# Values of 256 key rows by seven block products, in the setup of a graph-attention kernel

## The chip, the cores and the metric

The kernel runs on one core of a Trainium2 chip. The metric is device time in microseconds of one execution; a run lists several executions, and the median is used. The core's engines run side by side, each through its own queue in the order in which the program issues to it: TensorE (PE in the profile; PEld is its weight load), VectorE (DVE), ScalarE (ACT), GpSimd (POOL) and SyncE (SP, which here only issues DMAs). They wait for one another through semaphores. SBUF and PSUM are the on-chip memories; matmuls write to PSUM, and DVE or ACT copy from there.

## The reference

A graph-attention layer: 16 graphs of 512 nodes with 512 features, 16 heads of 32, and attention from every node to the first 20 nodes, in two directions (d = 0, 1).

```python
def _gat_attention(self_feat, cond_adj, label_bias, Wq, bq, Wk, bk, Wout, bout):
    B, N, F = self_feat.shape
    ng = min(NONGT, N)
    dh = F // H
    kv = self_feat[:, :ng]
    qh = (self_feat @ Wq.T + bq).reshape(B, N, H, dh)
    kh = (kv @ Wk.T + bk).reshape(B, ng, H, dh)
    aff = jnp.einsum('bnhd,bmhd->bnhm', qh, kh) * (1.0 / np.sqrt(dh))
    mask = cond_adj[:, :, None, :] > 0
    aff = jnp.where(mask, aff, NEG) + label_bias[:, :, None, :]
    w = jax.nn.softmax(aff, axis=-1)
    out_t = jnp.einsum('bnhm,bmf->bnhf', w, kv)
    out = jnp.einsum('bnhf,hgf->bnhg', out_t, Wout) + bout.reshape(H, F // H)
    return out.reshape(B, N, F)
...
        vcq = jnp.concatenate([exp_v, q_exp], axis=-1)
        self_feat = vcq @ W_self.T + b_self
        output = self_feat
        for d in range(2):
            ...
            output = output + _gat_attention(self_feat, cond, vb, Wq[d], bq[d], Wk[d], bk[d], Wout[d], bout[d])
        rel = jax.nn.relu(output)
        return exp_v + rel
```

The kernel exchanges the order of the last two products: it makes the values `kv @ Wout` of the 16 x 20 = 320 key rows once, in the setup, for both directions. Each is a product of 320 rows by 512 inputs with a 512 x 512 matrix. Half of `bout[0] + bout[1] + b_self` is added to the values of each direction.

## The kernel before

**Stages.** A setup (to about 86 us) loads the weights, makes the features of the 320 key rows (`kvn`, and `kvT` with its bias), the key vectors `khD`, the transformed keys `g` (16 head groups by 304 columns, stored to DRAM as `g_d`, the first two graphs kept in `gg`), the key biases `cq`, the values `vw_d`, and the first graph's own features. Then a loop over 16 graphs follows, in which PE makes scores, attention sums and the next graph's features. All matmuls are float32. A matmul of 64 or 32 output rows uses a part of PE's columns, so two or four of them run beside one another, and each float32 matmul leaves two records in the trace.

**Order.** The schedule is manual: the order of the calls in the program is the order in each engine's queue. The framework adds the semaphores, by tile and region; a tile taken from a pool again waits for all readers of the tile that held the buffer before.

**Rounds of the setup.** A loop over `n` = 0 to 12 (the last part of the listing) calls `keys(n)` and then the matmuls of one gap, by one letter each out of `plan[n]`. `keys(n)` issues a burst of small matmuls (line 949) on the tiles `s0`, `s1` and `t2` of PSUM, ordered by `bursts`, and the copies of their results to a tile `st`: ACT first (line 970), then DVE (line 972) and ACT (line 973). All three PSUM tiles have one buffer, so the next burst waits for these copies. Where a tile `st` is complete, POOL copies a part to `gg` (line 977) and SP stores the rest. The burst covers units (fc, hg, d, m), 46 of them in round 0, 41 in round 1, 46 in round 2; a unit needs `khD` of (d, hg).

The letters of a gap: `k` is `key_rows`, 16 matmuls whose result DVE copies to `khD` (line 850, `key_end`); `m` is `bias_terms`, a DVE product of `wq_sb` and `br_sb` with an accumulated sum (line 858); `v` and `w` are single steps of the values (line 902); `b` makes the biases `bqbd` on DVE and ACT; `c` is `bias_scores` (matmul, ACT copy, four POOL DMAs); `n` is `row_flags`; `p` is `block_product`, a block of the first graph's own features. Ahead of the loop four of the eight `key_rows` are made; the remaining four are (0, 2), (1, 2), (0, 3), (1, 3), in this order.

**Values before.** `values(t, ds, k)`: for each of the row blocks t = 0, 1 (128 rows) and each direction, four steps k over the 512 inputs, a step being two matmuls of 64 rows with 512 columns into one PSUM bank; then the last 64 rows with both directions in one bank. `value_pieces` adds the bias on DVE from the finished bank (line 918) and stores from POOL (line 922). The bias tile `br_sb` is completed on POOL at the end of round 2 by adding both rows of `bout` (line 1045), after the last `bias_terms` has read it.

**POOL ahead of the rounds.** `row_sums(0)` (lines 213 and 215) adds the four blocks of the first graph's `x`, which arrives during round 0, then `own_rows` and two copies to `c` follow, then the copies to `gg`.

**Buffers.** The pool `sfp`, tag `sf`, has three buffers: `wk0`, `wk1` and `kvD` hold them until the last `key_rows`; later come `rx1` (`row_sums(1)`, round 5), `sf0` and `t0` (round 8). The tag `adj` has three: `adj0_0`, `adj0_1`, the piece `v11`, then later masks. PSUM banks `acc0` and `acc1` (function `bank`) serve keys, values, bias scores, flags and block products in turn.

## Time and profile before

| | us |
|---|---|
| median of 3 executions | 544.9 |
| lowest, highest | 544.53, 545.13 |
| profiled execution, its own time | 546.22 |
| its span, first to last instruction | 544.2 |
| granted PE clock over the span | 0.997 |

Busy time by stage, in us of each stretch:

| stretch | PE | DVE | ACT | POOL | DMA share |
|---|---|---|---|---|---|
| 25 to 30 | 5.00 | 3.32 | 2.06 | 3.54 | 1.07 |
| 35 to 40 | 5.00 | 4.67 | 2.11 | 0.74 | 1.00 |
| 55 to 60 | 5.00 | 2.32 | 2.72 | 4.83 | 0.99 |
| 100 to 200 | 100.00 | 93.42 | 86.08 | 89.49 | 0.69 |
| 520 to 545 | 18.16 | 18.28 | 11.26 | 15.72 | 0.35 |

How to read it: a row of a timeline gives start, duration, engine, line, operation and the tiles written and read, with a count where neighbours are merged; in square brackets stands the idle time of that engine just before, and what ended it. A duration runs from an instruction's start on its engine to its end, so time for which it is held back on the engine is in it. The first and the last instructions of a stretch may be counted in two stretches. Times on POOL are rough.

### The profile page before, as it was taken

To read this page: it belongs to the slowest core of one execution; us is meant where nothing else is said; L and a number is where in the kernel's file an instruction comes from. 1 tells how busy PE (TensorE), PEld (TensorE's weight loads), DVE (VectorE), ACT (ScalarE), POOL (GpSimd) and SP (SyncE) were. 2 spreads that over 40 slices of the span, in tenths; PEclk is the share of its full clock that TensorE was granted. 3 is DMA by queue.
4 is the path that set the end of the run, shared out by engine and by line. 5 is a ranking of instruction groups with operands and counts; after the bars stand their busy time and mean duration, and the time that the engine had idled before them with its cause. 6 is when DMAs were issued, how large, how long until landed. Compare 5 with 4: busy or idle time off the path is not lost.

```text
span 544.2 us, 19643 instructions
## 1 busy us (share of the span) xinstructions
PE 537.1 (99%) x7932; PEld 427.1 (78%) x7932; DVE 472.3 (87%) x694; ACT 410.2 (75%) x1003; POOL 445.2 (82%) x447
## 2 busy tenths in 40 slices
PE   9999999999999999999999999999999999999995
PEld 5554469999887878887878788788888787888783
DVE  1785567899999999999999998999999999999996
ACT  1236646988887878797988888888888787877663
POOL 2657887679999897979797979898989989797584
PEclk9999999999999999999999999999999999999998
DMA  8999999476676877677767767576757676645024
GB/s 304 379 402 377 321 333 354 141 212 218 201 222 199 230 206 227 198 214 216 231 199 212 220 182 231 179 236 190 234 182 228 204 207 203 202 122 161 3 78 182
DMA packets 96182, 120.29 MB, mean 221 GB/s; under 512 B 20732, under 2 KB 64540, under 8 KB 94044
## 3 DMA queue, kind: packets, MB, share of 16 engines
q1 hardware_dynamic: 94748, 116.89, 67.9%
q0 software_dynamic: 768, 1.36, 1.2%
q8 instruction: 63, 1.03, 0.8%
q10 hardware_dynamic: 576, 0.79, 0.4%
q14 instruction: 27, 0.22, 0.2%
HBM read 83.41 MB, written 36.90 MB: 221 GB/s over the span
## 4 chain that ended last, share of the span: by engine, by line
PE 97%; DVE 1%; ACT 0%; issue 0%; DVEq 0%; ACTq 0%
PE ps_f L665 32%; PE ps_a L395 24%; PE ps_c L395 11%; PE ps_d L395 6%; PE ps_o_f L567 5%; PE ps_g L949 4%; PE ps_v L902 3%; PE ps_k L841 3%; PE ps_kv L784 2%; PE ps_a L282 1%; PE ps_o_c L567 1%; PE ps_l L395 1%; PE ps_c L282 1%; PE ps_kv L738 1%; PE ps_o_s L567 0%; PE ps_nz L220 0%
## 5 line engine op out<-in xcount | busy, mean ns | idle before, releaser
L325 ACT ACTIVATE prod<-adj,wb_sb 128x80 f32<-128x80 int32 x330 | 116.0, 429 | 0.0
L535 POOL TENSOR_TENSOR w<-w,sm 128x640 f32<-128x640 f32 x63 | 80.3, 1274 | 31.4 <-DVE sm L531 28.4
L665 PE MATMUL ps_f<-t,ws_s 128*64 128x246 f32 x720 | 80.1, 370 | 0.0
L665 PEld LDWEIGHTS ps_f<-t,ws_s 128*64 128x64 f32 x720 | 52.8, 136 | 18.0
L526 ACT ACTIVATE w<-w 128x640 f32<-128x640 f32 x60 | 43.8, 731 | 17.7 <-DVE w L522 17.7
L543 DVE STREAM_TRANSPOSE wt<-w 128x640 f32<-128x640 f32 x63 | 52.5, 833 | 0.1
L665 PE MATMUL ps_f<-x,ws_v 128*64 128x246 f32 x480 | 52.4, 371 | 0.0
L530 DVE TENSOR_REDUCE sm<-w 128x32 f32<-128x640 f32 x63 | 51.1, 811 | 0.1
L521 DVE TENSOR_REDUCE ps_d<-w 128x32 f32<-128x640 f32 x59 | 48.7, 826 | 1.8 <-ACT ps_d L429 0.2
L522 DVE TENSOR_TENSOR w<-w,ps_d 128x640 f32<-128x640 f32 x59 | 48.4, 821 | 2.0
L665 PEld LDWEIGHTS ps_f<-x,ws_v 128*64 128x64 f32 x480 | 35.4, 137 | 12.3
L368 POOL TENSOR_TENSOR k<-gg,k 128x608 f32<-128x608 f32 x30 | 44.7, 1489 | 0.0
L395 PEld LDWEIGHTS ps_a<-gg,sf 128*64 128x64 f32 x544 | 34.4, 137 | 5.8 <-issue 5.8
L970 ACT ACTIVATE st<-ps_g 128x448 f32<-128x448 f32 (+5 forms) x25 | 14.6, 642 | 32.1 <-PE ps_g L949 22.1
L395 PE MATMUL ps_a<-gg,sf 128*64 128x152 f32 x544 | 38.7, 295 | 0.0
L336 DVE TENSOR_REDUCE add<-prod 128x80 f32<-128x960 f32 x32 | 36.7, 1146 | 1.6 <-POOL prod L331 0.9
L395 PE MATMUL ps_d<-gg,sf 128*64 128x152 f32 x544 | 38.0, 293 | 0.0
L344 ACT COPY both<-add 64x80 f32<-64x80 f32 x128 | 32.6, 255 | 6.0 <-DVE add L336 4.9
L567 PE MATMUL ps_o_c<-wt,ve 32*32 32x256 f32 (+1 forms) x480 | 35.9, 386 | 0.0
L680 POOL TENSOR_TENSOR t<-x,t 128x492 f32<-128x492 f32 x30 | 34.9, 1162 | 1.2
L395 PEld LDWEIGHTS ps_d<-gg,sf 128*64 128x64 f32 x544 | 35.4, 137 | 0.2 <-ACT sf L683 0.2
L680 POOL TENSOR_TENSOR t<-x 128x492 f32<-128x492 f32 x30 | 34.9, 1164 | 0.0
(187 smaller groups left out, 1464.4 us busy)
## 6 DMA issues: line engine op xcount, KB each, us to landing
g_d<-st SPq DMA_DIRECT2D x16, 1064.0 KB
gg<-g_d SPq DMA_DIRECT2D x56, 304.0 KB
out_T<-o SPq DMA_DIRECT2D x60, 256.0 KB
x<-in_xT SPq DMA_DIRECT2D x56, 256.0 KB
xn<-in_xn SPq DMA_DIRECT2D x48, 256.0 KB
adj<-in_adj SPq DMA_DIRECT2D x52, 220.0 KB
nz<-nz_d SPq DMA_DIRECT2D x14, 256.0 KB
adj<-in_adj SPq DMA_DIRECT2D x6, 440.0 KB
```

The lines of the kernel that those rows point to most:

```text
L325: nc.scalar.activation(p[:, :, l], a[:, :, l], AF.Identity, scale=wb_sb[:, l : l + 1])
L368: done["ksum"] = engine.tensor_sub(to, one, two)
L395: nc.tensor.matmul(slot(g)[bass.ts(p, P // 2), : HL * S].rearrange("p (h m) -> p h m", m=NG)[:, :, 1:], of(k)[:, bass.ds(first + g * P // ...
L521: nc.vector.tensor_reduce(mx, f, AX.X, ALU.max)
L522: done["weigh"] = (engine or nc.vector).tensor_sub(f, f, mx.unsqueeze(2).to_broadcast([P, per, NG]))
L526: done["exp"] = nc.scalar.activation(t, t, AF.Exp)
L530: nc.vector.tensor_reduce(sm, heads(weighs[b, c, l]), AX.X, ALU.add)
L535: done["normal"] = nc.gpsimd.tensor_mul(f, f, smalls.pop((b, c, l)).unsqueeze(2).to_broadcast([P, per, NG]))
L543: done["turn"] = nc.vector.transpose(wts[b][:, c, l], weighs.pop((b, c, l)).rearrange("p g w -> p (g w)"))
L567: nc.tensor.matmul(outsum[b][a][bass.ds(at // 2 * DH, n * DH), bass.ds(c * N // 2 + lo * R, (hi - lo) * R)].rearrange("p (n r) -> p n r", ...
L665: nc.tensor.matmul(parts[b][n in (2, 3, 5)][bass.ts(a, P // 2), bass.ts(i, HN)], lhs, x[:, k], start=False, stop=k == 1, skip_group_check= ...
L680: done["xsum"] = nc.gpsimd.tensor_sub(to, one, two)
```

## The change

The first 256 key rows, with both directions at once, are one product of a 256 x 512 matrix (rows t = 0, 1; inputs in two halves j) with a 512 x 1024 matrix (halves j; directions d). Taken as 2 x 2 blocks, it is made by the seven products of Strassen's method in Winograd's form. Each product is two steps of two matmuls with 512 columns. It needs sums of blocks:

- `value_sums`: four sums of blocks of `kvT` on DVE, three in round 0 and one in round 1, right after `keys(n)`, of 256 columns each; three go into a new tile `kvS` of the tag `adj`, the fourth over a block of `kvT`.
- `weight_blocks`: four differences of blocks of `wo_sb`, 1024 columns each. Numbers 1, 2 and 4 run on POOL at the ends of rounds 1, 2 and 4, number 3 on DVE in two halves at the ends of rounds 3 and 4. They go into new tiles `wt0` and `wt1` of the tag `sf`.
- `value_product` accumulates product 2 in bank `acc1`, products 1, 6, 7, 4 one on another in `acc0`, and 5, 3 in a new `acc1`, in the order 2, 1, 5, 6, 3, 7, 4. `value_pieces` now runs once at the end of a round; it adds the bias into slices of a new tile `vs` (tag `sf`), joins the sums from PSUM on DVE, and stores.

The two rows of `bout` are added to one another on POOL at the end of round 1, and one sum completes `br_sb` in round 2. `bias_scores` is called in gaps 6 and 7 in place of 5 and 6. The warm-up matmuls at the start have 192 columns in place of 208. The last 64 rows are made as before.

```diff
+        kvS = load.tile([P, 2, S * L], F32, tag="adj", name="kvS", bufs=3)
+        kvS = kvS.rearrange("p t w -> p (t w)")[:, : 6 * P].rearrange("p (i k r) -> p i k r", i=3, k=2)
+        vx, vw = {}, {}
...
-            unit = nc.const_aps.tensor(1.0, [P, 208], F32)
+            unit = nc.const_aps.tensor(1.0, [P, 192], F32)
             for _ in range(4):
-                nc.tensor.matmul(warm[:, :208], unit[:, :P], unit, start=True, stop=True)
+                nc.tensor.matmul(warm[:, :192], unit[:, :P], unit, start=True, stop=True)
...
+            def weight_blocks(n, engine=nc.gpsimd, ks=slice(0, 2)):
+
+                b11, b21, b12, b22 = (wo_sb[d][:, 2 * j : 2 * j + 2] for d in range(2) for j in range(2))
+                if n == 1:
+                    t = [sfp.tile([P, C, F], F32, tag="sf", name=f"wt{i}") for i in range(2)]
+                    vw.update({1: b11, 2: b21, 3: b22, 5: t[0][:, :2], 6: t[0][:, 2:], 7: t[1][:, :2], 4: t[1][:, 2:]})
+                    vw["to"] = sfp.tile([P, C, F], F32, tag="sf", name="vs")
+                to, one, two = {
+                    1: lambda: (vw[5], b12, b11), 2: lambda: (vw[6], b22, vw[5]),
+                    3: lambda: (vw[7], b22, b12), 4: lambda: (vw[4], b21, vw[6]),
+                }[n]()
+                engine.tensor_sub(to[:, ks], one[:, ks], two[:, ks])
+
+            def value_sums(n):
+
+                a11, a12, a21, a22 = (kvT[:, 2 * j : 2 * j + 2, bass.ts(t, P)] for t in range(2) for j in range(2))
+                s1, s2, s4 = (kvS[:, i] for i in range(3))
+                if n == 0:
+                    nc.vector.tensor_add(s1, a21, a22)
+                    nc.vector.tensor_sub(s2, s1, a11)
+                    nc.vector.tensor_sub(s4, a12, s2)
+                else:
+                    nc.vector.tensor_sub(a21, a11, a21)
+                vx.update({1: a11, 2: a12, 3: s4, 4: a22, 5: s1, 6: s2, 7: a21})
+
+            def value_product(n, k):
+
+                first, i = n in (1, 2, 5), int(n in (2, 5, 3))
+                if first and k == 0:
+                    vw["ps", i] = bank(f"ps_v{n}", i)
+                for a in range(2):
+                    half = bass.ts(a, P // 2)
+                    nc.tensor.matmul(
+                        vw["ps", i][half], vx[n][:, k, half], vw[n][:, k],
+                        start=first and k == 0, stop=k == 1, skip_group_check=True,
+                    )
+                if k == 1:
+                    ended.append(n)
...
+                for n in sorted(done_now, key=(2, 1, 5, 6, 3, 7, 4, 0).index):
+                    if n == 2:
+                        with_bias(to[0], other)
+                    if n == 1:
+                        nc.vector.tensor_add(to[0], own_ps, to[0])
+                        store_values(to[0], 0, (0,))
+                    if n == 5:
+                        with_bias(to[1], other)
+                    if n == 6:
+                        with_bias(to[2], own_ps)
+                    if n == 3:
+                        nc.vector.tensor_add(to[2], other, to[2])
+                        store_values(to[2], 0, (1,))
+                    if n == 7:
+                        nc.vector.tensor_add(to[1], own_ps, to[1])
+                        store_values(to[1], 1, (1,))
+                    if n == 4:
+                        with_bias(to[3], own_ps)
+                        store_values(to[3], 1, (0,))
...
-                "v": [(values, (t, (d,), k)) for t in range(2) for d in range(2) for k in range(C)],
-                "w": [(values, (2, (0, 1), k)) for k in range(C)],
+                "v": [(value_product, (n, k)) for n in (2, 1, 5, 6, 3, 7, 4) for k in range(2)],
+                "w": [(values, (k,)) for k in range(C)],
             }
-            plan = "kmmk kmmmk mmmvvv vvv vvvb cvvv vvvc vnw www np pp pp pp".split()
+            plan = "kmmk kmmmk mmmvvv vvv vvvb vvv vvc cww wwn np pp pp pp".split()
...
                 keys(n)
+                if n < 2:
+                    value_sums(n)
...
-                    value_pieces()
                 if n == 2:
-                    for d in range(2):
-                        nc.gpsimd.tensor_add(br_sb, br_sb, bo_rows[d])
+                    nc.gpsimd.tensor_add(br_sb, br_sb, bo_rows[0])
+                value_pieces()
+                if n == 1:
+                    nc.gpsimd.tensor_add(bo_rows[0], bo_rows[0], bo_rows[1])
+                    weight_blocks(1)
+                if n == 2:
+                    weight_blocks(2)
+                if n in (3, 4):
+                    weight_blocks(3, nc.vector, slice(n - 3, n - 2))
+                if n == 4:
+                    weight_blocks(4)
```

`with_bias(v, ps)` is the DVE operation of line 918 (half of `br_sb` plus the bank), and `store_values(v, t, ds)` holds the POOL DMAs of line 922; both were parts of `value_pieces` before.

More of the change, by code (lines that the diff above doesn't have):

```diff
@@ L891, in gat_kernel @@
             ended = []
-            def values(t, ds, k):
+            def weight_blocks(n, engine=nc.gpsimd, ks=slice(0, 2)):
[9 more added lines that the diff above has]
+                engine.tensor_sub(to[:, ks], one[:, ks], two[:, ks])
@@ L896, in values, with store_values @@
+            def values(k):
+                if k == 0:
+                    vw["ps", 2] = bank("ps_v", 0)
+                for d in range(2):
+                    nc.tensor.matmul(
+                        vw["ps", 2][bass.ts(d, P // 2)], kvT[:, k, 2 * P :], wo_sb[d][:, k],
+                        start=(k == 0), stop=(k == C - 1),
+                    )
+                if k == C - 1:
+                    ended.append(0)
+            def store_values(v, t, ds):
                 rows = min(P, BM - t * P)
-                if k == 0:
-                    held[1 + t // 2] = bank(f"ps_v{t}{ds[0]}", int((t, ds) == (0, (1,))))
@@ L899, in values @@
-                ps = held[1 + t // 2]
                 for i, d in enumerate(ds):
-                    for a in range(2 * rows // P):
-                        nc.tensor.matmul(
-                            ps[bass.ds(i * rows + a * P // 2, P // 2)], kvT[:, k, bass.ds(t * P + a * P // 2, P // 2)], wo_sb[d][:, k],
-                            start=(k == 0), stop=(k == C - 1),
-                        )
-                if k == C - 1:
-                    ended.append((t, ds, ps))
+                    edge = EARLY * NG
@@ new lines, in store_values, with with_bias @@
+                    for n, lo, hi in ((0, 0, edge), (1, edge, rows)) if t == 0 else ((1, 0, rows),):
+                        nc.gpsimd.dma_start(
+                            vw_d[n][d, :, bass.ds(t * P + lo - n * edge, hi - lo)].rearrange("c r w -> r c w"),
+                            v[bass.ds(i * rows + lo, hi - lo)].rearrange("p (c w) -> p c w", c=C),
+                        )
+            def with_bias(v, ps):
+                nc.vector.scalar_tensor_tensor(v, br_sb, 0.5, ps, ALU.mult, ALU.add)
@@ L909, in value_pieces @@
             def value_pieces():
[L911 to L925 removed]
+                done_now = set(ended)
@@ new lines, in value_pieces @@
+                ended.clear()
+                to = [vw["to"][:, i] for i in range(C)] if "to" in vw else None
+                other, own_ps = vw.get(("ps", 1)), vw.get(("ps", 0))
+                for n in sorted(done_now, key=(2, 1, 5, 6, 3, 7, 4, 0).index):
[17 more added lines that the diff above has]
+                        store_values(to[3], 1, (0,))
+                    if n == 0:
+                        v = msk.tile([P, H * S], F32, tag="full", name="v2")[:, :F]
+                        with_bias(v, vw["ps", 2])
+                        store_values(v, 2, (0, 1))
```

15 lines of the change are left out of this document (removed).

## Prediction

> **What bounds the kernel now.** I read the page first, for which engine the chain of waits ends on.
>
> ```profile
> span 544.2 us, 19643 instructions
> PE 537.1 (99%) x7932; PEld 427.1 (78%) x7932; DVE 472.3 (87%) x694; ACT 410.2 (75%) x1003; POOL 445.2 (82%) x447
> PE 97%; DVE 1%; ACT 0%; issue 0%; DVEq 0%; ACTq 0%
> ```
>
> PE is busy for 99% of the span, and 97% of the chain lies on it. So a microsecond of matmul taken away counts in full, and a microsecond for which PE waits is added in full. Next I read PE's timeline where the values are made.
>
> ```profile
> 25.58 4.30 PE L841 MATMUL ps_k<-kvD,wk 128*32 128x304 f32 x64
> 29.81 1.39 PE L949 MATMUL ps_g<-khD,wq_sb 32*128 32x176 f32 x24
> 31.14 4.30 PE L841 MATMUL ps_k<-kvD,wk 128*32 128x304 f32 x64
> 35.37 1.54 PE L949 MATMUL ps_g<-khD,wq_sb 32*128 32x128 f32 x32
> 36.83 2.79 PE L902 MATMUL ps_v<-wo,kvT 128*64 128x512 f32 x12
> 39.56 1.66 PE L949 MATMUL ps_g<-khD,wq_sb 32*128 32x112 f32 x32
> 41.15 2.79 PE L902 MATMUL ps_v<-wo,kvT 128*64 128x512 f32 x12
> 43.88 1.63 PE L949 MATMUL ps_g<-khD,wq_sb 32*128 32x160 f32 x32
> ```
>
> Columns: start, duration, engine, line, matmul, count. Each row starts where the one before it ends: PE has no idle time here. Rounds alternate: a burst of key products (L949), then a gap (as the code calls it) of other matmuls. Round 1 begins at 29.81, round 2 at 35.37, round 3 at 39.56.
>
> **Matmuls removed.** Three steps of `values` (12 records) run from 36.83 to 39.56: 2.73 us, 0.91 a step. The sixteen steps for the first 256 rows become seven products of two steps with the same 512 columns: fourteen. Two steps go: **-1.82 us**. The last 64 rows keep four steps; bias scores change place, not count.
>
> **Warm-up.** 4 x 16 columns fewer.
>
> ```profile
> 0.84 3.11 PE L738 MATMUL ps_kv<-const-float32-1.0 128*128 128x208 f32 x8 [0.84 <-PEq L1421]
> 3.88 0.29 PEld L784 LDWEIGHTS ps_kv<-xkv,ws_v 128*64 128x64 f32 x4 [0.49 <-DMA ws_v<-in_wsT]
> ```
>
> The warm-up would be 3.11 x 16/208 = 0.24 us shorter, but the first real weights are loaded at 3.88, after 0.49 us of waiting for their DMA. The DMA stays: I count 0, bounds 0 and -0.24.
>
> **New work on DVE and POOL: how the two share.** The added sums take both inputs from SBUF, on both engines. The trace has that meeting.
>
> ```profile
> 25.34 1.22 DVE L972 TENSOR_SCALAR st<-ps_g 128x608 f32<-128x608 f32 x2 [0.63 <-PE ps_g L949]
> 26.30 1.28 POOL L213 TENSOR_TENSOR rx<-x 128x512 f32<-128x512 f32 x1 [4.27 <-DMA x<-in_xT]
> 27.67 2.96 POOL L215 TENSOR_TENSOR rx<-rx,x 128x512 f32<-128x512 f32 x2
> 27.91 0.59 DVE L850 TENSOR_SCALAR khD<-ps_k,bk_sb 128x304 f32<-128x304 f32 x1 [1.34 <-PE ps_k L841]
> 28.42 1.08 DVE L858 SCALAR_TENSOR_TENSOR bqt<-wq_sb,br_sb 128x512 f32<-128x512 f32 x1
> 29.43 1.75 DVE L858 SCALAR_TENSOR_TENSOR bqt<-wq_sb,br_sb 128x512 f32<-128x512 f32 x1
> L858 DVE SCALAR_TENSOR_TENSOR bqt<-wq_sb,br_sb x8: 680/686/1748, 28.4 to 38.9; 128x512 f32<-128x512 f32 x8
> 87.49 1.50 POOL L680 TENSOR_TENSOR t<-x 128x492 f32<-128x492 f32 x1
> 88.12 1.43 DVE L382 TENSOR_TENSOR f<-f,sf 128x512 f32<-128x512 f32 x1
> ```
>
> A `bqt` product takes 0.68 us (minimum of eight), but 1.75 at 29.43, ending only after POOL's sum does (30.63). At 88.12 a DVE sum whose first input was just made on DVE waits in the same way for POOL's, which ends at 88.99. So the two take turns, a whole instruction each, even where DVE's operations stand back to back. The khD copy, with one input in PSUM, keeps its 0.59 beside POOL's sums.
>
> [...]
>
> **First wait: three sums in round 0.** `value_sums(0)` is queued on DVE behind the eviction that ends at 26.56 and ahead of khD for (0, 2). That khD is read by the burst of round 1: round 0 takes the first 46 units, round 1 starts on the next, and its 11 shared ones are (0, 2). Before, khD ends at 28.50 for a burst at 29.81: 1.31 us to spare. Each sum has 256 columns. No row shows that size; the 512-column product runs in 0.68 and a 304-column sum in 0.69 with its tail. Bounds 0.2 and 0.69; I take 0.33, half of 0.68. Alone they would make 1.0 us and fit. But POOL makes the row sums from 26.30 on. The first waits until 27.59 and ends at 27.92; POOL takes 1.2 (29.12); the second ends at 29.45; POOL to 30.65; the third at 30.98; khD 0.59 to 31.57. Burst 1 starts near 31.6: **+1.8** (bounds 0.9, if DVE comes first, and 2.4).
>
> **Second wait: the weight sums in rounds 1 and 2.**
>
> ```profile
> 23.51 3.08 SPq L1029 DMA_DIRECT2D bo<-in_bout x2
> 32.90 0.82 POOL L977 COPY gg<-st 128x304 f32<-128x304 f32 x2
> 33.46 0.59 DVE L850 TENSOR_SCALAR khD<-ps_k,bk_sb 128x304 f32<-128x304 f32 x1 [0.64 <-PE ps_k L841]
> 36.50 1.22 DVE L972 TENSOR_SCALAR st<-ps_g 128x352 f32<-128x352 f32 x2
> 38.63 0.61 POOL L977 COPY gg<-st 128x304 f32<-128x304 f32 x1 [4.91 <-ACT st L973]
> 39.87 2.63 POOL L1045 TENSOR_TENSOR br_sb<-br_sb,bo 128x512 f32<-128x512 f32 x2 [0.64 <-DVE bqt L858]
> 42.73 0.69 DVE L918 SCALAR_TENSOR_TENSOR v<-br_sb,ps_v 128x512 f32<-128x512 f32 x1 [0.59 <-POOL br_sb L1045]
> ```
>
> POOL was idle for 4.91 us before 38.63, while DVE made five `bqt`s undisturbed. Into that idle time go one bias sum (half of 2.63: 1.28) and the first weight sum of 1024 columns. No row has 1024; twice 1.28 is 2.5, bounds 1.5 (the 608-column rate with a shorter tail) and 3.2. Their inputs, issued by 26.6, are read without a wait at 39.87; no row shows them late for POOL's turn, so I let them be there. Counted on from burst 1 at 31.6: it ends at 32.9, key products at 35.05 and 37.15, burst 2 at 38.6, three value steps at 41.33. On DVE: two `bqt`s, khD and the round's eviction to 34.6, the new sum to 34.95, khD to 35.75. POOL copies `gg` to 35.2 and makes the bias sum to 36.5; one `bqt` ends at 37.1; POOL makes the weight sum to 39.5; two `bqt`s and khD to 41.1; the eviction of burst 2 (1.22) ends at 42.35. Burst 3 writes the same PSUM and starts at 42.45 in place of 41.33: **+1.1**.
>
> Then come three `bqt`s with a `gg` copy (2.0, to 44.3), POOL's one remaining bias sum (to 45.7), 0.23 until DVE starts (42.50 to 42.73 in the rows), and the bias of the second product, 0.69, to 46.6. Product 5 takes that bank at once and could start at 44.96 (burst 3, one step): it starts near 46.7: **+1.75** (bounds of these two waits together 1.5 and 4).
>
> If round 1 isn't late, POOL's weight sum still stands between the `bqt`s: eviction of burst 2 at 41.3 for 39.56 (1.8), bias at 45.45 for a start at 43.9 (1.65): 3.45.
>
> **What I cost at nothing.** The biases of products 5, 6, 4 and the joins of 1, 3, 7 (0.69 each, one input in PSUM) end before their banks are wanted: two operations a round in a round of 4.3, of which evictions take 1.3. The two halves of the third weight sum on DVE (0.68 each) fall where POOL issues DMAs or copies; behind POOL's mask product they would cost up to 1.0. Weight sums two and four, 2.5 each, make POOL's queue longer:
>
> ```profile
> 72.42 1.15 POOL L255 TENSOR_TENSOR t<-x,t 128x492 f32<-128x492 f32 x1
> 74.37 1.83 PE L282 MATMUL ps_a<-t,ws_s 128*64 128x246 f32 x16
> ```
>
> The x sum for that product ends 0.8 us before it. POOL had gaps of 2.4 us ahead of it, and PE comes 2.8 us later by my sum: 0, with 0.8 as the upper bound. The row sums, x sum tiles and stores now share the `sf` buffers with the new tiles; the stores out of `vs` are issued two rounds before the tile is rewritten. Bias scores a round later have only stores behind them, which are read many rounds after. On SP nothing is moved.
>
> **Sum.** -1.82 + 1.8 + 1.1 + 1.75 = +2.8 us. The profiled execution took 546.2 us around its span of 544.2, and would take 549.0; the median of the three runs is 1.3 lower, 544.9, so I forecast **547.7**. Its own range is 546.2 to 549.2.
>
> **Rivals.**
> 1. *Only the weight sums collide.* The three sums slip in before POOL's. For: 0.25 us decides whether DVE or POOL is first at 26.3. Against: POOL was first, and x's landing is not moved. -1.82 + 3.45: 546.5.
> 2. *Only round 0 stalls.* POOL's weight sum finds a slot between evictions. Against: five `bqt`s in a row. -1.82 + 1.8: 544.9.
> 3. *Nothing stalls, the other side.* One mechanism: DVE keeps its turn while it has operations queued. Then the three sums end by 27.59 + 1.0 = 28.6 and khD by 29.2, and the `bqt`s end before the weight sum starts. It decides at khD by 29.7 and the second product's bias by 42. For: the sums alone fit the 1.34 us of idle time before khD. Against: the rows at 29.43 and 88.12. 543.1.
> [...]
> 5. *POOL's queue and the halves on DVE cost their bounds.* 0.8 + 1.0 more: 549.5.
>
> **Chances.** Forecast 0.50; rivals 0.14, 0.10, 0.17, 0.04, 0.05. Below 0.2% (1.1 us) a measurement of this kernel can't tell a change from none. Faster: rival 3, 0.17. Same: rival 2 and the low edge of rival 1, 0.13. Slower: the rest, 0.70. The range 544.5 to 549.7 leaves out rival 3 and little more.
>
> **What would show it.** In the changed kernel PE would wait before burst 1 for DVE's khD, before burst 3 for DVE's eviction, and in gap 3 for the bias of product 2; `value_sums` would show over 1 us where 0.33 is enough; fourteen value steps of 0.91 would stand. If the bursts still start at 29.81, 35.37 and 39.56, turn-taking is wrong and rival 3 holds.

## Result, and the profile after

| | before | after |
|---|---|---|
| median, us | 545.01 | 551.04 |
| lowest, highest, us | 544.53, 545.44 | 550.92, 552.34 |
| profiled execution, its span | 544.2 | 549.1 |
| granted PE clock | 0.997 | 0.994 |

The changed kernel is slower: ratio 1.0116, 95% interval 1.0099 to 1.0134. The forecast of 547.7 had the direction; the size is 6.0 us in place of 2.8, and the time lies outside the range. The page of the changed kernel, the lines that stood first in the prediction:

```profile
span 549.1 us, 19644 instructions
PE 537.9 (98%) x7924; PEld 426.9 (78%) x7924; DVE 485.4 (88%) x703; ACT 410.3 (75%) x1003; POOL 453.4 (83%) x450
PE 83%; POOL 3%; DVE 2%; issue 1%; ACT 0%; DVEq 0%; POOLq 0%
```

The eight records of the two removed steps are gone (7932 to 7924), yet PE is not busy for less time (537.1 to 537.9): some matmuls ran slower. And the span has grown by more than that, so PE waits. DVE has 13 us more busy time, far more than its new work: time in which an instruction was held is counted as busy. PE's timeline in the changed kernel shows where:

```profile
30.31 1.39 PE L1012 MATMUL ps_g<-khD,wq_sb 32*128 32x176 f32 x24
35.86 1.54 PE L1012 MATMUL ps_g<-khD,wq_sb 32*128 32x128 f32 x32
40.93 4.45 PE L928 MATMUL ps_v<-wo,kvT 128*64 128x512 f32 x12 [3.53 <-DVE khD L853]
45.31 1.66 PE L1012 MATMUL ps_g<-khD,wq_sb 32*128 32x112 f32 x32
47.81 1.89 PE L928 MATMUL ps_v<-wt,kvS 128*64 128x512 f32 x8
54.91 1.66 PE L1012 MATMUL ps_g<-khD,wq_sb 32*128 32x304 f32 x30 [0.52 <-DVE st L1035]
61.78 1.94 PE L928 MATMUL ps_v<-wt,kvT 128*64 128x512 f32 x8 [0.63 <-DVE vs L980]
80.93 1.88 PE L282 MATMUL ps_a<-t,ws_s 128*64 128x246 f32 x16 [0.54 <-POOL t L255]
```

Bursts 1 and 2 start 0.50 and 0.49 later than before without a wait; burst 0 does too (24.48 for 23.99 in the two timelines), so this comes from ahead of the rounds. Then, in gap 2, PE waits 3.53 us for a copy of `khD`, ahead of product 2. The three steps behind it take 4.45 us, where the same twelve records took 2.79 before. Burst 3 starts at 45.31 in place of 39.56, 5.75 late; the rest is small waits. The windows of the same kernel say why the steps are slow (window; busy time and count of PE, PEld, DVE, ACT, POOL; granted clock, DMA share, GB/s):

```profile
40.00:41.00 1.00, 0.07 (x2) 0.07 (x4) 1.00 (x4) 0.00 (x0) 0.00 (x0) 0.95 1.02 377
41.00:42.00 1.00, 1.00 (x4) 0.38 (x6) 1.00 (x3) 0.00 (x0) 0.44 (x1) 0.50 0.64 238
43.00:44.00 1.00, 1.00 (x4) 0.24 (x2) 0.84 (x4) 0.00 (x0) 0.02 (x1) 0.50 1.18 423
45.00:46.00 1.00, 1.00 (x18) 0.69 (x20) 0.69 (x1) 0.00 (x0) 1.00 (x2) 1.00 0.77 260
```

After the idle time of 3.53 us the granted clock is 0.50 from 41 to 44 us. What held the copy is read from two timelines of the changed kernel. POOL's:

```profile
27.52 1.47 POOL L213 TENSOR_TENSOR rx<-x 128x512 f32<-128x512 f32 x1 [5.00 <-DMA x<-in_xT]
35.61 1.44 POOL L1111 TENSOR_TENSOR bo<-bo,bo 128x512 f32<-128x512 f32 x1 [0.23 <-DMA bo<-in_bout]
37.01 2.80 POOL L907 TENSOR_TENSOR wt<-wo,wo 128x1024 f32<-128x1024 f32 x1
```

And DVE's:

```profile
26.98 0.41 DVE L914 TENSOR_TENSOR kvS<-kvT 128x256 f32<-128x256 f32 x1
27.89 1.39 DVE L916 TENSOR_TENSOR kvS<-kvT,kvS 128x256 f32<-128x256 f32 x1
35.86 1.75 DVE L861 SCALAR_TENSOR_TENSOR bqt<-wq_sb,br_sb 128x512 f32<-128x512 f32 x1
37.53 2.83 DVE L861 SCALAR_TENSOR_TENSOR bqt<-wq_sb,br_sb 128x512 f32<-128x512 f32 x1
40.29 0.58 DVE L853 TENSOR_SCALAR khD<-ps_k,bk_sb 128x304 f32<-128x304 f32 x1
50.35 3.30 DVE L907 TENSOR_TENSOR wt<-wo 128x512 f32<-128x512 f32 x1
55.45 2.85 DVE L907 TENSOR_TENSOR wt<-wo 128x512 f32<-128x512 f32 x1
```

Two `bqt` products of 0.68 us take 1.75 and 2.83, behind POOL's bias sum and its weight sum. The `khD` copy of (1, 3) stands behind them on DVE and ends at 40.87; it reads the bank `acc1`, which product 2 takes next. The halves of the third weight sum take 3.30 and 2.85 in place of 0.68.

The account, by PE's positions against before: +0.5 until burst 0, +3.5 before product 2, +1.7 from the halved clock, +1.0 around burst 5 (0.52 and a held start, behind the first half), +0.8 before product 4 (behind the second half, by way of the join of product 7), +0.6 at the block product, -1.8 for the two steps: 6.3, as PE's last matmul is 6.25 later (544.09 for 537.84). The span grew by 4.9 only, since in the profiled execution of before more time passes after the last matmul.

### The profile page after: what moved, and what is told of

It is laid out like the page before. It is cut to its first block, busy times and chain, and to the rows that moved or that the text cites. A ratio compares the mean times of both kernels' runs of the same rounds, so it can differ in the third digit from the quotient of the medians.

```text
span 549.1 us, 19644 instructions
## 1 busy us (share of the span) xinstructions
PE 537.9 (98%) x7924; PEld 426.9 (78%) x7924; DVE 485.4 (88%) x703; ACT 410.3 (75%) x1003; POOL 453.4 (83%) x450
## 4 chain that ended last, share of the span: by engine, by line
PE 83%; POOL 3%; DVE 2%; issue 1%; ACT 0%; DVEq 0%; POOLq 0%
PE ps_f L665 32%; PE ps_a L395 24%; PE ps_c L395 11%; PE ps_d L395 6%; PE ps_o_f L567 5%; PE ps_o_c L567 1%; PE ps_a L282 1%; POOL vw_d L952 1%; PE ps_l L395 1%; POOL cq_d L889 1%; PE ps_c L282 1%; PE ps_g L1012 1%; POOL rx L215 0%; PE ps_o_s L567 0%; POOL t L255 0%
```

## Experiments

### The changed kernel again, and the warm-up

No edit (e12):

> The changed kernel unchanged, beside the next two on one chip. [...] Rival (the cost is fixed, 551.0): all executions within 1 us of 551.

549.94 us (548.21 to 551.43), ratio 1.009 (1.007 to 1.011). The same wait in its profile, and no slow steps behind it:

```profile
41.03 2.79 PE L928 MATMUL ps_v<-wo,kvT 128*64 128x512 f32 x12 [3.53 <-DVE khD L853]
```

The granted clock here is 1.00 in each of the windows from 41 to 44 us, where the first profile has 0.50. So the clock is halved in some executions and not in others, after the same idle time: the executions of this run with a mean clock of 0.994 and 0.995 took 550.5 to 551.4, those of 0.996 to 0.999 took 548.2 to 549.4. The wait is shown apart from the clock, and by these times I estimate the clock at some 2 us.

In this profile PE's last matmul is 3.7 us later than before, against 6.25 in the changed kernel's first profile. That is more than the 1.7 of the slow steps: burst 5 doesn't wait either. With burst 3 earlier by those 1.6 us, the first half of the third weight sum comes up early in POOL's issue of two DMAs; in the first profile it comes up near the end of that issue, with POOL's mask product next. DVE's row of e12, then POOL's:

```profile
48.80 0.68 DVE L907 TENSOR_TENSOR wt<-wo 128x512 f32<-128x512 f32 x1
```

```profile
48.15 1.73 POOL L952 DMA_DIRECT2D vw_d<-vs  x2
```

It takes 0.68 here and 3.30 in the first profile. Of the profiles whose rounds 3 to 5 make the sums as in the changed kernel, the three with slow steps (the first one, e1, e6) have 3.30 to 3.33 and a wait of 0.52 to 0.55 at burst 5, and the others (e2, e5, e11, e12, e16) have 0.68 or 0.69 and none. So the 1.0 around burst 5 goes with the clock; what remains without it is the wait before product 2, the 0.8 before product 4 and the x sum.

The warm-up alone, in the kernel before (e3), and undone in the changed one (e1):

```diff
-            unit = nc.const_aps.tensor(1.0, [P, 208], F32)
+            unit = nc.const_aps.tensor(1.0, [P, 192], F32)
```

> The kernel before with the warm-up of 192 columns alone. [...] Rival (chance): no difference beyond 0.3 us.

> The changed kernel with the warm-up of 208 columns back. [...]

e3: 544.84 against 544.98, ratio 1.000 (0.9991 to 1.0008): the warm-up does nothing that can be measured. e1: 549.70 (547.05 to 552.04), ratio 1.0078 (1.0052 to 1.0105). Its profile shows the first wait, which the changed kernel's does not. DVE's timeline, then PE's:

```profile
26.54 1.43 DVE L914 TENSOR_TENSOR kvS<-kvT 128x256 f32<-128x256 f32 x1
28.00 1.39 DVE L915 TENSOR_TENSOR kvS<-kvS,kvT 128x256 f32<-128x256 f32 x1
29.43 1.38 DVE L916 TENSOR_TENSOR kvS<-kvT,kvS 128x256 f32<-128x256 f32 x1
```

```profile
31.46 1.39 PE L1012 MATMUL ps_g<-khD,wq_sb 32*128 32x176 f32 x24 [1.51 <-DVE khD L853]
40.90 4.49 PE L928 MATMUL ps_v<-wo,kvT 128*64 128x512 f32 x12 [2.35 <-DVE khD L853]
```

Here POOL's row sums started at 26.41, as `x` had landed, ahead of DVE's sums, and each of the three waited for one of POOL's: 1.4 us in place of 0.4. In the changed kernel's profile they started at 27.52 and only the third waited. But product 2 starts at the same moment in both, 40.90 and 40.93: that moment is set by POOL's weight sum, and what PE waits before burst 1 it no longer waits before product 2. And behind 2.35 us of idle time the three steps take 4.49; the mean granted clock from 24 to 60 us is 0.95, as in the changed kernel's profile (1.00 in before).

### What makes PE wait before product 2

The three sums ahead of burst 0 (e6, whose edit follows), and the first weight sum as two instructions of 512 columns, between which a DVE product can run (e2):

```diff
+            value_sums(0)
             for n in range(len(bursts)):
...
-                if n < 2:
+                if n == 1:
                     value_sums(n)
```

> The changed kernel with the three sums of round 0 moved ahead of the burst of round 0, where POOL is idle. Theory (the waits of rounds 1 and 2 hang on POOL's weight sum, which starts when its data and its turn come, about 36.3 to 37.0 us, whatever PE does before; the wait of round 1 is only taken out of the next one): the wait before burst 1 is gone in every execution, PE waits about 3.5 us before product 2, the clock falls to 0.5 there. Time 550.7, bounds 549.5 and 551.5. Rival (the waits add up, as the prediction had it): the time falls by what burst 1 waited, 1.5 us in the profile of the first run, to 549.5 or less.

> The changed kernel with the first weight sum on POOL as two instructions of 512 columns in place of one of 1024. [...] Time 548.2, bounds 547.5 and 549.0. Rival (the wait is set by late data of the weights, not by turns): PE still waits 3.5 us, the clock still falls to 0.5, 551.0.

e6: 547.64 (546.00 to 550.77), ratio 1.0048 (1.0027 to 1.0069). The theory expected next to no gain on the changed kernel, and there are 2 to 3 us of it: a miss, and the rival (549.5 or less, since the waits add up) has the number. The profiled execution is its slowest, at a clock of 0.994, and speaks for the theory: no wait before burst 1, and product 2 starts at 40.79 after 2.89 of waiting, as late as without the edit. How the faster executions save is not shown. e2: 546.91 (546.21 to 550.95), ratio 1.0053 (1.0029 to 1.0076). In its profile the wait before product 2 is 0.61 and the three steps take 2.79; 0.56, 0.60, 0.63 and 0.98 are waited elsewhere. Two of its six executions, at a clock of 0.995, took 549.83 and 550.95. A shorter turn on POOL removes most of the wait.

The two PSUM banks exchanged among the values, so that product 1 and not product 2 follows `khD` (1, 3) in its bank (e5):

```diff
-                first, i = n in (1, 2, 5), int(n in (2, 5, 3))
+                first, i = n in (1, 2, 5), int(n not in (2, 5, 3))
...
-                other, own_ps = vw.get(("ps", 1)), vw.get(("ps", 0))
+                other, own_ps = vw.get(("ps", 0)), vw.get(("ps", 1))
```

> The changed kernel with the two PSUM banks of the products exchanged, so that product 2 takes the bank of key block (0, 3), which is copied early, and product 1 that of (1, 3). Theory (the 3.5 us are a wait for that bank): PE makes product 2 at once and then waits some 1.7 us before product 1; no idle time reaches 3 us, the clock stays at 1.00 throughout; then it waits about 1.5 us for the bias of product 2, which DVE makes no earlier than in the changed kernel (45.3 us). Time 549.3, bounds 548.5 and 550.2. Rival (PE waits there for the operands of product 2, not for its bank): wait of 3.5 us and clock of 0.5 as in the changed kernel, 551.0.

548.79 (547.69 to 549.00), ratio 1.0066 (1.0053 to 1.0079), within the bounds of the theory. The rows of product 1 and product 5:

```profile
40.92 1.08 PE L928 MATMUL ps_v<-wo,kvT 128*64 128x512 f32 x4 [0.48 <-DVE khD L853]
46.02 1.94 PE L928 MATMUL ps_v<-wt,kvS 128*64 128x512 f32 x8 [1.31 <-DVE vs L958]
```

No wait before product 2, and no slow step (granted clock 1.00 from 24 to 60 us); 0.48 before product 1, and product 5 now waits 1.31 for the bias of product 2, the wait that the prediction priced at 1.75. The bank is what PE waited for.

Six more matmuls in the idle time (e11; 2.73 us of work whose results are overwritten; they take the bank of product 1, which then doesn't take it anew):

```diff
+                if n == 2:
+                    vw["ps", 0] = bank("ps_v1", 0)
+                    for _ in range(3):
+                        for p in range(2):
+                            rows_p = bass.ts(p, P // 2)
+                            nc.tensor.matmul(
+                                vw["ps", 0][rows_p], kvT[:, 0, rows_p], wo_sb[0][:, 0], start=True, stop=True,
...
```

> The changed kernel with six more matmuls of 512 columns (three value steps, 2.7 us) ahead of product 2, into the free bank, their results overwritten. Theory (PE's clock is halved because PE is idle before product 2, which costs 1.7 us): the granted clock stays at 1.00 through the value steps, which take 2.7 us in place of 4.4; the wait for the bank shrinks to under 1 us; although PE has 2.7 us more to do the time falls by up to 1.7 against the changed kernel on this chip, to about 549.5. Rival (the halved clock has nothing to do with the idle time): value steps as slow as before, no fall, or a rise by up to 2.7.

548.91 (546.67 to 549.67), 1.0 us below e12 beside it (the intervals, 1.0050 to 1.0088 and 1.007 to 1.011, overlap). In its profile the added matmuls run from 37.42, product 2 follows at 40.26 without a wait, and its three steps take 2.80. Work of 2.7 us that costs nothing shows that the time before product 2 was idle.

### The sums apart: two by two

Three kernels leave out work of the changed one. e15 makes no sums of the weights (products 5, 6, 7 and 4 read blocks of `wo`), e16 not the three sums of values in round 0 (products 3, 5 and 6 read blocks of `kvT`), e17 neither. The edit of e15:

```diff
-                    vw.update({1: b11, 2: b21, 3: b22, 5: t[0][:, :2], 6: t[0][:, 2:], 7: t[1][:, :2], 4: t[1][:, 2:]})
+                    vw.update({1: b11, 2: b21, 3: b22, 5: b12, 6: b22, 7: b12, 4: b21})
...
-                engine.tensor_sub(to[:, ks], one[:, ks], two[:, ks])
+                pass
```

> The changed kernel without the four sums of the weights (POOL's three of 1024 columns and VectorE's two of 512): products 5, 6, 7 and 4 read blocks of wo as loaded; the three sums of values stay. Theory (the sums of the weights make the wait before product 2, those of product 7 and of the block product, and the idle time after which the clock is halved): no wait before product 2, none over 0.3 us between 35 and 90 us, and only the wait before burst 1, between 0 and 1.8 us as x or VectorE's sums come first: 544.9 - 1.8 + 0 to 1.8 = 543.1 to 544.9 us. Rival (the joins and biases, one gap later, or the stores wait by themselves): 546 us and more, with waits of 0.5 us and more after 35 us.

> The changed kernel without the three sums of values in the first round (products 3, 5 and 6 read blocks of kvT in their place); the four sums of the weights stay. Theory (the wait before product 2 is set by POOL's weight sum and the bqt behind it, whatever came before): no wait before burst 1, 2.5 to 3.6 us before product 2 at 37 to 41 us, and 548 to 551 us, as in the changed kernel; it gains under 1 us on it. Rival (the three sums put VectorE behind, and the later waits follow from that): under 546.5 us.

> The changed kernel without the sums of the weights and without the three sums of values: the products, biases, joins and stores alone. Theory (two steps of 0.91 us less, and nothing else on the path): no wait of TensorE over 0.3 us between 24 and 90 us, and 544.9 - 1.8 = 543.1 us, bounds 542.6 and 543.7. Rival (the saving is given back elsewhere, by the later biases or by the loop, which waits for something else): 544.5 us and more.

| | weight sums | no weight sums |
|---|---|---|
| value sums | 1.009 and 1.0116 (e12, first run) | 1.0019 (1.0010 to 1.0028) |
| no value sums | 1.0041 (1.0027 to 1.0054) | 1.0002 (0.9993 to 1.0012) |

The medians are 545.68 (545.05 to 546.31) for e15, 546.85 (546.18 to 547.12) for e16 and 544.97 (544.09 to 545.51) for e17, beside 544.65 for before. Over before, the value sums alone leave 1.0 us, the weight sums alone 2.2, both together 5.0 and 6.0 in their two runs. The theory missed on all three.

In e15 PE waits 1.40 before product 2 though no weight sum is made. DVE's timeline:

```profile
35.81 1.76 DVE L861 SCALAR_TENSOR_TENSOR bqt<-wq_sb,br_sb 128x512 f32<-128x512 f32 x1
37.50 0.68 DVE L861 SCALAR_TENSOR_TENSOR bqt<-wq_sb,br_sb 128x512 f32<-128x512 f32 x1
38.11 0.58 DVE L853 TENSOR_SCALAR khD<-ps_k,bk_sb 128x304 f32<-128x304 f32 x1
```

The product behind POOL's bias sum (35.75 to 37.02) is held as in the changed kernel; the next one is not. The difference between its 0.68 and the 2.83 there, 2.15, is that between the waits, 1.40 and 3.53, within 0.02. This is what the weight sum alone does. In e16 PE waits only 1.07 before product 2: without the held sums DVE is 0.6 us earlier, its third `bqt` (35.85 to 37.59) takes the turn ahead of POOL's weight sum, and the `khD` copy follows at once. In the changed kernel that third `bqt` came up at 37.53, 0.5 us after POOL had begun. Half a microsecond decides over 2.5.

The greatest miss is e17: without the sums the saving of 1.8 is gone all the same. Its PE timeline:

```profile
37.86 2.80 PE L926 MATMUL ps_v<-wo,kvT 128*64 128x512 f32 x12 [0.61 <-DVE khD L853]
46.62 2.79 PE L926 MATMUL ps_v<-wo,kvT 128*64 128x512 f32 x12
74.69 1.88 PE L282 MATMUL ps_a<-t,ws_s 128*64 128x246 f32 x16 [0.84 <-POOL t L255]
```

The first comes from the bias sum that POOL now makes at 34.94, on a `bqt` at 35.54 that takes 1.75. The second is POOL's x sum, which ends at 74.63, where it ended at 73.57 before. With 0.35 at the start that is the whole saving. Had the x sum kept its time, PE would have found it ready here; but even then it left the matmuls only 0.8 us to gain. It is 1.06 later as POOL's store of the last 64 rows, which stands ahead of it, begins at 68.97 in place of 67.94. By the order of POOL's queue this comes from the second bias scores, which the change calls a gap later: their last DMA is issued only at 67.59, after 0.93 of idle time. e18 was to test this, and met another wait:

> The kernel of e17_no_sums with both steps of the bias scores in the same gap, the sixth, where e17 has the second of them a gap later (it can't go sooner: the bank is the products' until then). The sums of the weights and the three of values are left out as in e17. In e17 POOL's x sum for the block product ends at 74.63 us, 1.06 later than before, and TensorE waits 0.84 for it. Theory (the stores of the second bias scores, issued a gap later than before, stand ahead of the last values' stores and of the x sum on POOL): the x sum ends some 0.8 us sooner, the wait falls under 0.2 us, and the time from 545.0 to 544.1 us, bounds 543.7 and 544.5. Rival (the x sum waits for the biases of the last 64 rows on VectorE, which the scores don't hold up): a wait of 0.6 us or more, 544.7 to 545.3 us.

e18 is e17 with the bias scores in one gap:

```diff
-            plan = "kmmk kmmmk mmmvvv vvv vvvb vvv vvc cww wwn np pp pp pp".split()
+            plan = "kmmk kmmmk mmmvvv vvv vvvb vvv vvcc ww wwn np pp pp pp".split()
```

550.04 (548.14 to 550.50), ratio 1.0086 (1.0070 to 1.0102): the opposite of what was expected, and a cause that I had not thought of. POOL's timeline, then a row of PE's:

```profile
66.33 0.80 POOL L950 DMA_DIRECT2D vw_d<-vs  x1
70.11 2.11 POOL L322 TENSOR_TENSOR prod<-prod,wb_sb 128x880 f32<-128x880 f32 x1
75.90 1.05 POOL L255 TENSOR_TENSOR t<-x 128x492 f32<-128x492 f32 x1 [3.69 <-DMA vw_d<-vs]
```

```profile
78.22 2.53 PE L282 MATMUL ps_a<-t,ws_s 128*64 128x246 f32 x16 [3.40 <-POOL t L255]
```

The x sum's tile `t0` takes over the buffer of `vs`, and by the profile waits until the last store out of `vs`, issued at 66.33, has landed; e21 below tests this. In e18 that store is issued 2.7 us later than in e17 (63.60), behind eight DMAs of the bias scores in place of four. The matmuls behind the wait are slow again (2.53 for 16 records that take 1.88; the clock row of the page has 8 tenths in the slice from 68.5 to 82.2 us).

### Arrangements of the whole change

e8: the value sums and two `bias_terms` ahead of burst 0, the bias of values completed in round 1 in the buffer of `bout`, the third weight sum whole on DVE in round 2, POOL's second mask product behind the x sums, and fewer `bias_terms` beside the weight sums. e9 is e8 with the third sum in halves as in the changed kernel, e10 is e8 with the value sums back behind burst 0.

```diff
-            plan = "kmmk kmmmk mmmvvv vvv vvvb vvv vvc cww wwn np pp pp pp".split()
+            plan = "kmmk kmkm vvv mvvv mvvv vvvb vvc cww wwn np pp pp pp".split()
...
+                    nc.gpsimd.tensor_add(bo_rows[1], bo_rows[0], bo_rows[1])
+                    nc.gpsimd.tensor_add(bo_rows[1], br_sb, bo_rows[1])
```

> The changed kernel with its work on DVE and POOL rearranged, no operation left out: the three sums and two of the eight key bias products ahead of burst 0; one key bias product less in gap 1 and the others in gaps 3 and 4; the bias of the values in a tile of its own, so that it doesn't wait for those products; the third weight sum as one operation in round 2; the x sums of round 8 ahead of the mask product. Theory (all that the seven products lost, they lost to turn-taking of DVE and POOL): no wait of PE over 0.3 us between 24 and 90 us, two value steps fewer; time 543.4, bounds 542.8 and 544.6, so 0.1 to 0.4% below the kernel before. Rival (the products themselves cost more, by bank changes or by their operands): waits of PE at the value steps remain, 545 or more.

> The rearranged kernel with the third weight sum on DVE in two halves at the ends of rounds 3 and 4 again, as in the changed kernel. Theory (there each half waits for POOL's mask product and for the fourth weight sum, 3.3 and 2.8 us in place of 0.6, and DVE's next eviction comes late): bursts 5 and 6 and the step after them wait 1.0 to 1.8 us in all; time 544.9, bounds 544.0 and 545.6. Rival (those waits only fill time that PE would lose anyway): within 0.3 us of the rearranged kernel.

> The rearranged kernel with the three sums of round 0 behind the burst of round 0 again, as in the changed kernel. Theory (whether they wait depends on the moment x arrives; with nothing behind it that waits anyway, the wait of burst 1 now counts): burst 1 waits 0 to 1.8 us, from execution to execution; median 1.0 above the rearranged kernel, 544.4, bounds 543.4 and 545.3, and a wider spread. Rival: no difference beyond 0.3 us.

e8: 547.61 (545.45 to 549.10), ratio 1.0046 (1.0029 to 1.0063), a miss. The profiled execution, its best, waits 1.28 before burst 1 and 0.46 for the x sum; all others had a clock of 0.992 to 0.994, and their waits are not recorded. e9: 546.42 (545.16 to 547.34), 1.0022 (1.0013 to 1.0031). e10: 546.04 (544.62 to 548.47), 1.0024 (1.0008 to 1.0040). e9 and e10 were expected to be slower than e8 and are not: misses too. The wait before product 2 is gone in all three profiles, of which each caught the fastest execution of its run; others of 0.2 to 1.5 stay.

e13 also loads `wo` and `bout` ahead of `x`, makes the bias in round 0, weight sums 1 and 2 in round 1 and POOL's row sums at the end of round 2:

```diff
-            load_x(0)
-            nc.sync.dma_start(wb_sb, w_bias.partition_broadcast(P))
-            load_adj(0, 0)
...
+            bo_rows = [load.tile([P, N], F32, tag="nz", name=f"bo{d}") for d in range(2)]
+            for d in range(2):
+                nc.sync.dma_start(bo_rows[d], bout[d : d + 1].partition_broadcast(P))
+            load_x(0)
...
+            plan = "kmmmk kkm vvv mvvv mvvv vvvb vvc cww wwn np pp pp pp".split()
```

> The rearranged kernel with its loads in another order, no operation left out: wo and bout ahead of x and the masks; the row sums of x on POOL at the end of round 2; the bias sums in round 0, weight sums 1 and 2 in round 1; key bias products 2 ahead of burst 0, 3 in gap 0, 1 behind the last copy of gap 1, one each in gaps 3 and 4. Theory (what makes the rearranged kernel lose in most executions is that x, wo or bout come late, so that sums on POOL still meet DVE's sums and PE's idle time halves its clock): no wait of PE over 0.3 us between 24 and 70 us, granted clock 1.00 there, 543.6, bounds 542.8 and 544.8, and a spread under 1.5 us. Rival (the spread comes from elsewhere): 546 to 548 with a spread of 3 us as before.

547.10 (546.86 to 547.73), ratio 1.0041 (1.0029 to 1.0053). No wait until 50 us, then one of 2.85 at 54.13, for the bias of a product that stands behind this row of DVE's timeline; POOL's rows of the same time follow it:

```profile
46.77 6.69 DVE L863 SCALAR_TENSOR_TENSOR bqt<-wq_sb,br_sb 128x512 f32<-128x512 f32 x1
```

```profile
45.99 1.73 POOL L954 DMA_DIRECT2D vw_d<-vs  x2
47.74 2.11 POOL L322 TENSOR_TENSOR prod<-prod,wb_sb 128x880 f32<-128x880 f32 x1
49.77 0.83 POOL L1042 COPY gg<-st 128x304 f32<-128x304 f32 x2
50.55 2.35 POOL L909 TENSOR_TENSOR wt<-wo,wt 128x1024 f32<-128x1024 f32 x1
```

One product of 0.68 us, up since 46.77, gets no turn until POOL's queue pauses at 52.9. The granted clock is 0.82 from 52 to 56 us and 0.76 from 56 to 60; the expectation of full clock and 543.6 failed on it. e14 moves this product into gap 0 (plan `kmmmmk kkm vvv mvvv vvv vvvb ...`):

> The kernel of e13_data_first, with the two products of POOL's and VectorE's fourth stretch exchanged for others so that no VectorE product is queued there: the product that took 6.69 us in e13 goes into the stretch before burst 0, where POOL has little to do. Theory (what is left in e13 is the one product that got no turn, 2.85 us of waiting of TensorE at 54.13 and the clock of .82 and .76 after it, some 1.4 us): no wait of TensorE over 0.5 us between 24 and 70 us, and 547.1 - 2.85 - 1.4 = 542.9 us, bounds 542.3 and 544.2, faster than before. Rival (some other VectorE operation with two inputs loses its turns to POOL in its place, since the same POOL work has still to go through in the same time): a wait of 1 to 3 us elsewhere between 30 and 60 us, and 545 to 547 us. Third case (the product in the stretch before burst 0 delays the first evictions): a wait before burst 1 of over 1 us and 544 to 546 us.

547.82 (545.85 to 548.02), ratio 1.0047 (1.0031 to 1.0063). As the theory had it, PE doesn't wait between 24 and 70 us, and the granted clock is 1.00 there. But then it waits for the x sum, and the x sum for the last store out of `vs`. PE's row, then POOL's:

```profile
76.43 1.88 PE L282 MATMUL ps_a<-t,ws_s 128*64 128x246 f32 x16 [3.23 <-POOL t L255]
```

```profile
74.12 1.05 POOL L255 TENSOR_TENSOR t<-x 128x492 f32<-128x492 f32 x1 [3.35 <-DMA vw_d<-vs]
```

This is e18's cause, hidden until nothing else was late. So the time did not move. e21 gives the values of the last product another buffer:

```diff
-                        with_bias(to[3], own_ps)
-                        store_values(to[3], 1, (0,))
+                        v = msk.tile([P, H * S], F32, tag="full", name="v10")[:, :F]
+                        with_bias(v, own_ps)
+                        store_values(v, 1, (0,))
```

> The kernel of e14_gap4, with the last product's values (rows 128 to 255, direction 0) in a tile of the ring that the last 64 rows' values use, in place of the fourth part of vs. In e14 POOL's x sum waits 3.35 us for the store of that fourth part, issued at 63.43 and landed at 74.1, since the x sum's tile takes over the buffer of vs; TensorE waits 3.23 for it. Theory (the reused buffer is the cause): the x sum follows the store of the last 64 rows at 70.8 and ends at 73.0, as TensorE comes to it; the wait of 3.23 goes, the one of 0.92 for the third x sum stays: 547.5 - 3.2 = 544.3 us, bounds 543.6 and 545.2. Rival (POOL's x sum is late by its own queue): a wait of 1 us or more at 73 us, 545.3 to 547 us.

> The kernel of e21_own_tile, with the third x sum issued on POOL ahead of the second mask product (2.1 us) in place of behind it. Theory (with the buffers apart, what is left is 0.92 us of waiting for the third x sum): no wait of TensorE over 0.3 us between 24 and 90 us, and 543.4 us, bounds 542.7 and 544.2, below the kernel before. Rival (the mask product, 1.2 us later, holds up the copies gg and the mask's use in the loop): a wait of 0.5 to 1.5 us after 85 us, 544 to 545 us.

e21: **543.70** (543.31 to 545.16), ratio 0.9981 (0.9972 to 0.9990), 1.25 us below the 544.95 of before. Its only waits between 20 and 130 us are these, and the profiled execution, 545.02, is one of its slower ones:

```profile
73.81 1.88 PE L282 MATMUL ps_a<-t,ws_s 128*64 128x246 f32 x16 [0.57 <-POOL t L255]
78.21 1.88 PE L282 MATMUL ps_a<-t,ws_s 128*64 128x246 f32 x16 [0.92 <-POOL t L255]
```

e22, with the third x sum ahead of the mask product, loses both, has 0.76 at 86 us in their place (for ACT's copy of `ps_a`), and takes 544.13 (542.92 to 545.26), ratio 0.9986 (0.9976 to 0.9996): no further gain. Both beat the kernel before, so the products pay in this arrangement. The two kernels also load `wo` and `bout` earlier and move other work of POOL and DVE. Whether the kernel before would gain by the same reordering was not tried, so the 1.25 us is not shown to come from the products alone.

## Why the prediction was right or wrong

The sum was -1.82 + 1.8 + 1.1 + 1.75 = +2.8, and the account of the first profile is +6.3. The 3.5 between them are 1.7 (halved clock), 1.0 and 0.8 (the two halves of the third weight sum), 0.6 (x sum) and 0.5 (start), less 1.1 by which the three waits, 4.65 in all, were priced too high against the 3.53 that PE waited.

- **The step that failed: a wait of PE was priced by its length alone, so the clock is missing from the sum.** It said that "a microsecond for which PE waits is added in full", and added nothing else. Behind the 3.53 us PE's granted clock stood at 0.50 from 41 to 44 us and the three steps took 1.7 longer; burst 5 lost 1.0 more, as it does in the three profiles with slow steps ahead of it and in none of the five without. In e12 the same kernel, after the same wait, has neither cost in its profile, and its three executions at a mean clock of 0.996 and above, 548.2 to 549.4, lie within the range that the prediction gave. All four executions of the first run have 0.993 or 0.994 and lie outside. I had looked for the clock only at the start, with a chance of 0.04 for a slow stretch that lasts longer behind the shorter warm-up. No run shows the 1.5 us counted for it: the block of matmuls there takes 7.59 us in e3's profile and 7.02 in before's, but the time of e3 doesn't move, ratio 1.000; and the windows of before have a granted clock of 1.00 from 0.8 to 11.8 us, also where a matmul takes 701 ns, so that stretch is not shown to be the clock's at all.
- **Second wait: in the wrong place.** The prediction let burst 2 end and the three value steps follow at 38.6 without looking at what they need. Product 2 needs the bank of `khD` (1, 3), and that copy stands on DVE behind the products that were just made late: by the prediction's own times at 41.1, and measured at 40.87. I priced the lateness at burst 3, 1.1, where its eviction ends; PE met it three value steps earlier, in one piece. On the prediction's own times the bank would have cost 2.5 before product 2, taken the 1.1 away and left 0.35 of the 1.75: the same 4.65, since the last of the waits sets the total. So the place did not spoil the sum; it hid that PE would stand still for long at once, after which the clock fell.
- **Third wait, +1.75 before product 5:** 0 in the changed kernel, as product 2 itself is late; 1.31 in e5, where it is not. The mechanism stands, its place in the sum does not.
- **First wait, +1.8: a matter of a microsecond.** e1 shows it, 1.51; the changed kernel's profile has none, as POOL's row sums start 1.2 us later than in before and two of DVE's sums slip in ahead of them. That is rival 1, whose 3.45 for the rest is close to the 3.53 by luck: it adds a wait at burst 3 to one before product 5, and neither came. And the first wait must not be added to the second: product 2 starts at 40.9 either way.
- **Turn-taking of DVE and POOL: right.** The products took 1.75 and 2.83, the sums 1.4, as by whole instructions. Which of the two goes first is not settled by that: in e13 a product that stood ready was passed over for POOL instructions that came up later, 6.69 us in all.
- **The matmuls, -1.82: right.** Where the granted clock is 1.00 the steps take 0.91, fourteen of them. That PE's time counts in full was only half the truth: POOL's x sum left 0.8 us, and in e17 it came later still. I had the 0.8 as a bound for the price of the weight sums, not as the end of the gain.
- **At nothing:** the halves on DVE cost 1.8 in the first profile and 0.8 where the granted clock stayed at 1.00 (e12; rival 5 had 1.0 for both), the 0.8 by way of a join, of which the prediction said that all end in time. The x sum cost 0.6 (rival 5 had 0.8). The shared `sf` buffers cost nothing in the changed kernel, but 3.2 in e14, where a store out of `vs` had not landed: the sentence that such stores are issued two rounds ahead looked at the issue and not at the landing.
- **The weight sum's size:** 2.5 was taken, and 2.36 (number 2) and 2.80 (number 1, beside DVE's product) were measured. The lower bound of 1.5 does not follow from the rows of 608 columns: 1.48 x 1024/608 is 2.5.
- **Profiled time against median:** the 1.3 us between them were the profiled execution's own; the median of before came out at 545.0 again.

What decides in which executions the clock falls stays open; so do how the gain of e6 over the changed kernel comes about and which waits the slower executions of e8 have, since the profiles caught other executions. What issue or landing ends POOL's idle time before its eighth bias-score DMA (1.27 to 2.27 us in e14, e21 and e22, by the profile the landing of an earlier one) was not tried.

## What to carry to other kernels

When an engine is made late, walk down its queue to the first result that PE needs, and ask of each matmul for its bank as well as for its inputs; the first wait takes away from the next, so waits are placed in time and not added up. A long wait of PE can have a second price besides its length, that of the clock behind it: here 1.7 us for the steps behind 3.53 us of waiting in the first profile, and none in e12. A saving on the bounding engine lasts only until the next engine's chain: look up how early each of its inputs is ready before counting the saving in full. A rearrangement that moves the wait shows the next one; here the saving appeared only with the turns, the queue order and one buffer all put right.

## What the runs showed of the hardware

- **A ready DVE product can lose several turns.** 6.69 us in e13: from the issue of two POOL DMAs at 46.0 through a mask product, two copies and a weight sum.
- **It matters how far POOL's DMA issue has come.** While POOL issued two stores (1.73 us), DVE operations of 512 columns with both inputs in SBUF that started 0.27 to 0.66 us into the issue took 0.68 or 0.69 (e2, e5, e9, e11, e12, e16). Those that started 0.78 us (e13) and 1.10 us (the changed kernel, e1, e6) into it were held past its end, for 6.69 and 3.30 to 3.33 us. Why is not shown.
- **The clock after idle time is not a matter of its length alone.** Behind 3.53 us PE's granted clock was 0.50 in the changed kernel and 1.00 in e12, each from 41 to 44 us. The mean from 24 to 60 us was 0.95 in the profiles with waits of 2.35 us (e1), 2.85 (e13), 2.89 (e6) and 3.53 (the changed kernel) in that stretch, and 1.00 in e12. After 3.40 us (e18) 16 records took 2.53 and the 32 of the burst behind them 2.56; after 3.23 us (e14) the same took 1.88 and 1.66. What decides is not shown.
- **A store from POOL takes long to land.** 9.6 us from its issue at 66.33 to the release at 75.90 in e18, 10.7 in e14 (63.43 to 74.12).
